# Two buffers for the weights of the wavelet layer's products, paid for with the GpSimd descriptor ring

## The chip, the cores and the metric

The kernel runs on one core of one Trainium2 chip. The metric is the device time of one execution in microseconds. Three executions of the kernel before took 18142.69, 18163.43 and 18164.18 us; the median is 18163.43 us.

A core has TensorE (PE in the profile; PEld is its loading of weights), VectorE (DVE), ScalarE (ACT), GpSimd (POOL) and SyncE (SP). All work from fast memory of 128 partitions (SBUF); products go to PSUM. Each engine takes its own instructions in order. SP and POOL start transfers; 16 DMA engines carry them.

## The reference

The input is `x` of 8 images, 64 channels, 128 x 128, float32. Four layers follow each other, each as `x = x + layer(groupnorm(x))`:

```python
x = x + relu(b - sum |patch - w|)         # layer 0: 3x3 "adder" convolution, 64 channels out
x = x + scale * silu(x) + spline(x)       # layer 1: per channel, B-spline
x = x + idwt(gelu(conv3x3(conv1x1(dw3x3(haar(x))))))   # layer 2: wavelet layer, 256 channels at 64 x 64
x = x + embed[argmin |x - embed|^2]       # layer 3: nearest of 512 vectors
```

Layer 0 has no product in it: for each output it sums 576 absolute differences.

## The kernel before

**Pairs.** Two images (64 channels each) fill the 128 partitions, so there are four pairs. Layer 0 is by far the longest. For pair 0 it runs alone; then one long run of layer 0 does pairs 1, 2 and 3, and beside it the layers 1, 2 and 3 of the pair before are done in small steps (`beside`, L1736). The last pair's layers 1 to 3 come at the end with nothing beside them.

**Layer 0** (L548 on). A tap is one shift of a 32-row chunk against one output channel's weight. ACT makes `|x - w|` of a tap (L821), or DVE makes `max(x, w)` (L774) and may fold a second and third tap into it (L844); PE sums the tile over channels into PSUM with a selection matrix (L809). A tile is 128 x 4096 floats, 16 KB of a partition. While the program is built, `layer0` keeps a clock of each engine from fixed costs, hands taps to ACT or DVE by it, and so writes the order of all engines out by hand; nothing of it is decided while the chip runs. There is a second way to fold two DVE taps, the *merge* (L832): POOL starts a transfer that adds one tile to another in SBUF (`accum_op=ALU.add`), 2 MB, and PE later takes the sum. The policy `ALONE` (pair 0) merges; `BESIDE` has its threshold `merge_free` at 99 and never does. After each pass of 144 taps ACT writes `y` (L645), eight POOL transfers add the layer's input to it (`residual`, L658, 64 KB each), and SP stores it (L673). The planner counts a merge as landed 12.5 us after it begins (`MERGE`), and plans its use by PE 5 or 9 us after that (`SETTLED`, `UNSETTLED`).

**Layer 2 beside layer 0** (`layer2_beside`, L1416). `spread_out` runs events by step: `at(step, f, ...)`. There are 514 steps to a pair, and chunks of 16 rows that are 56 steps apart. For chunk `c` that begins at step `b`, PE does sixteen groups of 24 matmuls (`products`, L1507, the matmuls at L1516), with the steps `b + 14 * at_m + 3 + 3 * n`: four kinds of product `at_m`, four groups each, three steps between groups of a kind and five from one kind to the next. Each group needs its own 384 KB of weights, tile `u2`, loaded from DRAM by SP (`load_u2`, L1503, L1505). The profile writes this tile as `u`. The pool has `bufs=1`, so there is one `u2` tile in this layer: a load waits until the group before it is done with the tile. A load stands one step behind the group before its own; the first of a chunk stands at `b - 3`.

**SP's queue.** SP is not ordered by hand, but takes its transfers in the program's order, and one that waits holds those behind it. In this layer these are the input rows `xin` (L1456, one buffer, free when DVE's `rows` of the part before are done), the residual rows `xa` (L1563, stored at L1579 after DVE's `add`), layer 0's stores of `y` (L673, each waiting for `residual` to land), small ones for layer 0's linear part (L621, L631, L635), and the weights (L1505).

**POOL's transfers.** Merges, `residual` and layer 3's gathers (L1687, L1245) go through POOL, which writes their descriptors into a ring in SBUF. `dynamic_dma_scratch_size` is the ring's size in bytes of each partition: 4096.

Of the kernel before, what the change touches and what calls it, by code (L numbers as in the profile page):

```python
# [13 lines left out]
F32 = mybir.dt.float32  # L14
# [7 lines left out]
P = 128  # L22
# [76 lines left out]
class Net:  # L99
# [1316 lines left out]
    def layer2_beside(self, stats_in, stats, steps):  # L1416
# [3 lines left out]
        nc, tc = self.nc, self.tc  # L1420
# [6 lines left out]
        def at(step, f, *a):  # L1427
            events[step].append((f, *a))

        with ExitStack() as ctx:  # L1430
            sp = ctx.enter_context(tc.tile_pool(name="b2", bufs=1))
# [20 lines left out]
            xins, vs, mms, gs, pys, u2s, xas = {}, {}, {}, {}, {}, {}, {}  # L1452
# [48 lines left out]
                nc.vector.tensor_tensor(vs[c, m], d[a], d[z], op)  # L1501

            def load_u2(c, m, oab, half):  # L1503
                t = u2s[c, m, oab, half] = sp.tile([P, 2, 3, P], F32, name="u2")
                nc.sync.dma_start(out=t, in_=self.u2_dram[:, oab, m, 2 * half : 2 * half + 2])  # L1505

            def products(c, m, oab, half):  # L1507
# [76 lines left out]
            for j in range(NCH + 1):  # L1584
                b, each = (7, LEAD) if j == 0 else (7 + LEAD + EACH * (j - 1), EACH)
                if j < NCH:
                    lo, row = (2 * G * j + 4, 2) if j else (0, 0)
                    hi = min(2 * G * (j + 1) + 4, H)
                    for h, s in enumerate((-5, -2, 1, 4) if j else range(0, 10, 2)):
                        to = min(lo + G // 2, hi)  # L1590
                        if lo == to:
                            continue
                        at(max(b + s - 3, 0), load, j, h, lo, to)
                        at(b + s + 1, columns, j, h, to - lo)
                        if h == 0 and j > 0:
                            at(b + s + 2, halo, j)
                        at(b + s + 2, rows, j, h, to - lo, row)
                        row += (to - lo) // 2
                        lo = to
                    for n in range(36):  # L1600
                        at(b + 7 + n * (each - 10) // 36 if j else b + 11 + n * (each - 14) // 36, depthwise, j, n)
                    at(b + each - 2, border, j)
                if j >= 1:
                    c = j - 1
                    kinds = ((1, take_first), (0, take_second), (2, take_third), (3, take_fourth))
                    when = [(b + 14 * at_m + 3 + 3 * n, c, m, n // 2, n % 2) for at_m, (m, _) in enumerate(kinds) for n in range(4)]
                    for n, (step, *what) in enumerate(when):
                        at(when[n - 1][0] + 1 if n else b - 3, load_u2, *what)
                        at(step, products, *what)
                    for at_m, (m, take) in enumerate(kinds):  # L1610
                        at(b + 14 * at_m, columns_of, c, m)
                        at(b + 14 * at_m + 15, take, c)
                    for oab in range(2):
                        at(b + 58, gelu, c, oab)
                    for a in range(2):
                        s = b + 60 + 9 * a
                        at(s - (8 if a == 0 else 1), load_x, c, a, 0)
                        for n in range(2):
                            at(s + n, inverse, c, 2 * a + n)
                        for h in range(2):  # L1620
                            for n in range(2):
                                at(s + 3 + 4 * h, add, c, 2 * a + n, h)
                            at(s + 3 + 4 * h, store, c, a, h)
                        at(s + 4, load_x, c, a, 1)
# [165 lines left out]


# [13 lines left out]
```

## Time and profile before

| | us |
|---|---|
| median of three executions | 18163.43 |
| profiled execution, whole | 18174.13 |
| its span, first to last instruction | 18172.4 |
| PE busy | 17725.0 (98%) |
| DVE busy | 17665.0 (97%) |
| ACT busy | 17155.7 (94%) |
| POOL busy | 3450.7 (19%) |
| pair 0, layer 0 alone | about 160 to 3640 |
| layer 0 of pairs 1 to 3, other layers beside it | about 3640 to 16900 |
| of that, matmuls of `products` | 4706 to 6140, 9200 to 10990, 13760 to 15516 |
| last pair's layers 1 to 3 | about 16900 to 18172 |

"Busy" counts time in which an engine runs an instruction; idle time is put down to what ended it, "who waited for whom". For PE and DVE all idle time together is 447 and 507 us of the span, and it comes in single waits of some microseconds. A row of the timeline gives start, duration, engine, line, operation, tiles and, in brackets, the idle time before it with its releaser.

### The profile page before, as it was taken

How to read it: one execution, taken by the hardware profiler on the slowest of the kernel's cores; microseconds unless marked ns; L12 is line 12 of the kernel's file. 1: busy time of each engine (PE TensorE's matmuls, PEld its weight loads, DVE VectorE, ACT ScalarE, POOL GpSimd, SP SyncE). 2: the span in 40 equal slices, each digit the busy share in tenths (PEclk: the TensorE clock that was granted, in tenths of full speed). 3: DMA queues.
4: the chain of work that ended last, by engine and by line, in shares of the span. 5: the costliest groups of instructions: out<-in, count | busy, mean ns of one | idle time of the engine just before them, and what ended most of it. 6: DMA issues, size and time to landing. Idle time of an engine off the chain costs nothing.

```text
span 18172.4 us, 338264 instructions
## 1 busy us (share of the span) xinstructions
PE 17725.0 (98%) x150466; PEld 6115.0 (34%) x150466; DVE 17665.0 (97%) x13415; ACT 17155.7 (94%) x6554; POOL 3450.7 (19%) x1866
## 2 busy tenths in 40 slices
PE   8999999999999999999999999999999999999999
PEld 2222222222333332332233333333223333333365
DVE  8999999999999999999999999999999999999998
ACT  7999999999999999999999999999999999999925
POOL 1222222200000024440000002453000000244305
PEclk9999999999999999999999999999999999999998
DMA  6767767711111110011111111001111111110231
GB/s 144 133 125 137 137 126 127 145 43 39 44 49 52 45 41 26 23 32 36 40 43 48 51 46 41 26 23 32 39 41 41 48 53 43 29 29 21 61 103 56
DMA packets 454215, 1099.93 MB, mean 61 GB/s; under 512 B 72416, under 2 KB 234848, under 8 KB 395360
## 3 DMA queue, kind: packets, MB, share of 16 engines
q0 software_dynamic: 111792, 491.89, 15.2%
q1 hardware_dynamic: 340960, 586.39, 11.1%
q8 instruction: 1179, 19.32, 0.4%
q14 instruction: 284, 2.33, 0.0%
HBM read 526.58 MB, written 125.74 MB: 36 GB/s over the span
## 4 chain that ended last, share of the span: by engine, by line
PE 51%; DVE 27%; issue 11%; ACT 8%; DMA 2%; POOL 0%; SPq 0%; DVEq 0%; ACTq 0%; POOLq 0%
PE ps L809 39%; DVE buf L774 13%; ACT buf L821 6%; DVE buf L844 4%; PE mm L1516 4%; PE pd L1672 1%; PE m L1080 1%; DVE dw L1489 1%; DVE wide L774 1%; DVE r L1358 1%; DMA buf<-buf 1%; PE ps L1230 1%; DVE x L844 1%; DVE x L774 1%; ACT t L1674 1%
## 5 line engine op out<-in xcount | busy, mean ns | idle before, releaser
L809 PE MATMUL ps<-buf,sel 128*32 128x512 f32 x112944 | 12564.7, 594 | 142.6 <-ACT buf L821 57.8
L821 ACT ACTIVATE buf<-wide,w 128x4096 f32<-128x4096 f32 x1898 | 6918.7, 3724 | 58.1 <-PE ps L809 57.6
L821 ACT ACTIVATE buf<-x,w 128x4096 f32<-128x4096 f32 x1820 | 6637.6, 3717 | 76.8 <-PE ps L809 71.9
L809 PEld LDWEIGHTS ps<-buf,sel 128*32 128x32 f32 x112944 | 3547.9, 110 | 8589.2 <-issue 7829.1
L774 DVE TENSOR_SCALAR buf<-x,w 128x4096 f32<-128x4096 f32 x1807 | 4183.6, 2358 | 55.5 <-PE ps L809 45.4
L774 DVE TENSOR_SCALAR buf<-wide,w 128x4096 f32<-128x4096 f32 x1737 | 4041.4, 2368 | 34.8 <-PE ps L809 30.6
L1687 POOL DMA_INDIRECT g<-in_L_conv_embed_weight,ix x768 | 1885.3, 2455 | 2322.9 <-issue 1188.2
L658 POOL DMA_DIRECT2D y<-in_x x496 | 702.9, 2230 | 6852.5 <-ACT y L645 5454.4
L844 DVE SCALAR_TENSOR_TENSOR buf<-x,w,buf 128x4096 f32<-128x4096 f32 x417 | 1870.2, 4485 | 14.8
L844 DVE SCALAR_TENSOR_TENSOR buf<-wide,w,buf 128x4096 f32<-128x4096 f32 x409 | 1834.2, 4485 | 14.5
L1516 PE MATMUL mm<-v,u 64*128 64x256 f32 x9216 | 1147.1, 393 | 76.2 <-DMA u<-u_dram 60.3
L832 POOL DMA_DIRECT2D buf<-buf x203 | 546.5, 2694 | 2713.2 <-DVE buf L774 2321.0
L1516 PEld LDWEIGHTS mm<-v,u 64*128 64x128 f32 x9216 | 871.9, 190 | 485.2 <-issue 299.4
L821 ACT ACTIVATE x<-wide,w 128x4096 f32<-128x4096 f32 x266 | 990.2, 3722 | 6.4 <-PE ps L809 6.4
L821 ACT ACTIVATE wide<-x,w 128x4096 f32<-128x4096 f32 x260 | 966.7, 3718 | 2.8 <-PE ps L809 2.7
L809 PE MATMUL ps<-x,sel 128*32 128x512 f32 x7760 | 928.3, 594 | 4.8 <-DVE x L844 4.4
L809 PE MATMUL ps<-wide,sel 128*32 128x512 f32 x7664 | 917.2, 593 | 8.5 <-ACT wide L821 5.5
L1489 DVE SCALAR_TENSOR_TENSOR dw<-sub,dws,dw 128x512 f32<-128x512 f32 (+2 forms) x768 | 573.5, 747 | 11.0
L1674 ACT ACTIVATE t<-emb,xsq 128x512 f32<-128x512 f32 x768 | 516.6, 727 | 39.1 <-DVE best L1684 28.7
L1684 DVE CUSTOM_DVE_ANT_0 nd<-pd,t 128x512 f32<-128x512 f32 x768 | 520.2, 677 | 23.2 <-ACT t L1674 14.3
L1686 DVE FIND_INDEX8 ix<-best,nd 128x8 uint32<-128x512 f32 x768 | 526.4, 685 | 0.1
L774 DVE TENSOR_SCALAR wide<-x,w 128x4096 f32<-128x4096 f32 x219 | 516.8, 2360 | 6.6 <-PE ps L809 6.6
(286 smaller groups left out, 10591.1 us busy)
## 6 DMA issues: line engine op xcount, KB each, us to landing
buf<-buf POOLq DMA_DIRECT2D x203, 2048.0 KB, 15.7
u<-u_dram SPq DMA_DIRECT2D x512, 384.0 KB
z<-x_dram SPq DMA_DIRECT2D x192, 256.0 KB
x<-x_dram SPq DMA_DIRECT2D x96, 512.0 KB
raw<-in_x SPq DMA_DIRECT2D x32, 1024.0 KB
x_dram<-y SPq DMA_DIRECT2D x512, 64.0 KB
y<-in_x POOLq DMA_DIRECT2D x496, 64.0 KB, 5.1
x_dram<-x SPq DMA_DIRECT2D x48, 512.0 KB
```

Source lines behind the costliest of these rows:

```text
L658: nc.gpsimd.dma_start(out=ys[p][at], in_=d, accum_op=ALU.add)
L774: nc.vector.tensor_scalar(ab, tap(p // OG, t), w[:, t : t + 1], None, ALU.max)
L809: nc.tensor.matmul(to, sel[:, M - 1 - m : 3 * M - 1 - m], rhs, start=(done % TAPS == 0), stop=((done + span) % TAPS == 0))
L821: nc.scalar.activation(ab, tap(p // OG, t), AF.Abs, bias=w[:, t : t + 1], scale=-1.0)
L832: nc.gpsimd.dma_start(out=into, in_=of, accum_op=ALU.add, max_dma_last_dim=8192)
L844: nc.vector.scalar_tensor_tensor(ab, tap(p // OG, t), w[:, t : t + 1], ab, ALU.max, ALU.add)
L1489: nc.vector.scalar_tensor_tensor(out, v, wt, out, ALU.mult, ALU.add)
L1516: nc.tensor.matmul(ps[:, i], u2[r, k % 2, di, :], vs[c, m][r, k, di : di + G, :], start=(k == 0 and di == 0), stop=(k == 3 and di == 2))
L1674: nc.scalar.activation(t, emb[:, 1], AF.Identity, bias=xsqs[j][:, n : n + 1])
L1684: nc.vector.tensor_tensor_reduce(nd, ps, t, 1.0, -FAR, ALU.subtract, ALU.max, mx[:, 0:1])
L1686: nc.vector.max_index(ix, mx, nd)
L1687: nc.gpsimd.indirect_dma_start(out=g[:, img, :], out_offset=None, in_=self.embed, in_offset=bass.IndirectOffsetOnAxis(ap=ix[:, 0:1], axis=0),)
```

## The change

`u2` gets two buffers in the layer beside layer 0. Each load moves one group ahead: it stands one step behind the group two before its own, and the first two of a chunk stand at `b - 5` and `b - 4`. A buffer is 2 x 3 x 128 floats, 3072 bytes of a partition. The ring of POOL's descriptors goes from 4096 to 1024 bytes of a partition, which frees 3072.

```diff
             def load_u2(c, m, oab, half):
-                t = u2s[c, m, oab, half] = sp.tile([P, 2, 3, P], F32, name="u2")
+                t = u2s[c, m, oab, half] = sp.tile([P, 2, 3, P], F32, name="u2", bufs=2)
                 nc.sync.dma_start(out=t, in_=self.u2_dram[:, oab, m, 2 * half : 2 * half + 2])
...
                     for n, (step, *what) in enumerate(when):
-                        at(when[n - 1][0] + 1 if n else b - 3, load_u2, *what)
+                        at(when[n - 2][0] + 1 if n > 1 else b - 5 + n, load_u2, *what)
                         at(step, products, *what)
...
-    nc = bacc.Bacc("TRN2", target_bir_lowering=False, num_devices=1, dynamic_dma_scratch_size=4096)
+    nc = bacc.Bacc("TRN2", target_bir_lowering=False, num_devices=1, dynamic_dma_scratch_size=1024)
```

## The prediction

> **What bounds the kernel now.** First the stretches of the two stages that the change touches: layer 0 alone (pair 0), where all merges are, and the three stretches with `products`.
>
> ```profile
> 160.00:3640.00 3480.00, 3428.33 (x31548) 1018.77 (x31540) 3422.90 (x1429) 3409.49 (x969) 773.28 (x332) 1.00 0.73 132
> 4706.00:6140.00 1434.00, 1413.91 (x12520) 562.05 (x12520) 1419.94 (x887) 1404.40 (x419) 47.41 (x44) 0.99 0.18 50
> 9200.00:10990.00 1790.00, 1756.43 (x15503) 694.74 (x15502) 1757.96 (x1055) 1739.24 (x517) 59.42 (x52) 0.99 0.17 47
> 13760.00:15516.00 1756.00, 1728.04 (x15300) 688.04 (x15292) 1735.15 (x1030) 1720.15 (x511) 75.78 (x58) 0.99 0.17 48
> ```
>
> After each length come the busy times of PE, PEld, DVE, ACT and POOL. PE and DVE are both about 98.5% busy: PE idles 52 us of the first stretch and 82 us of the other three together, DVE 57 and 67. The reader is to see that neither stage has one bound: time given to PE counts only as far as DVE was waiting for it. So I read the waits next: PE's, DVE's for the time beside other layers (3640 to 16900), and POOL's neighbours.
>
> ```profile
> PE mm L1516 <- DMA u<-u_dram: 60.3, 28, 6.7
> PEld mm L1516 <- DMA u<-u_dram: 90.1, 33, 7.6
> PE ps L809 <- DMA buf<-buf: 28.7, 5, 10.5
> ...
> DVE buf L774 <- PE ps L809: 48.9, 26, 14.8
> ```
>
> Of 384 groups of `products`, 33 start late because their weights have not landed; PE idles 60 us there. The merges already cost PE 28.7 us. Then the timeline at one of the 33:
>
> ```profile
> 9649.29 2.41 PE L1516 MATMUL mm<-v,u 64*128 64x256 f32 x20
> 9659.25 0.32 SPq L1456 DMA_DIRECT2D xin<-x_dram  x1
> 9659.67 0.37 SPq L1505 DMA_DIRECT2D u<-u_dram  x1
> 9662.93 4.55 PE L1516 MATMUL mm<-v,u 64*128 64x256 f32 x24 [4.23 <-DMA u<-u_dram]
> ```
>
> The buffer was free at 9651.7, but SP stood before `xin`, whose buffer DVE freed at 9659.2; the weights went out behind it and landed 3.2 us later. The 24 matmuls then take 4.55 us in place of 2.86: after a long wait PE runs slow for a while. Last the merges:
>
> ```profile
> L832 POOL DMA_DIRECT2D buf<-buf x203: 1201/2211/22579, 141.2 to 3599.1; - x102
> DMA to landing us min/median/max: 14.6/15.7/35.2
> ...
> 1386.31 1.95 POOL L832 DMA_DIRECT2D buf<-buf  x1 [13.88 <-PE ps L809]
> 1399.79 2.21 POOL L832 DMA_DIRECT2D buf<-buf  x1 [11.53 <-DVE buf L774]
> ...
> q0 software_dynamic: 272, 2.10, 81.2%
> ```
>
> A merge lands 15.7 us after POOL begins it, and here the next begins after 13.5 us. The last line is the window of one merge, 1388 to 1402.5: 272 packets, which by size are 256 of 8192 B and 16 of 4 B, 17 for each of 16 DMA engines.
>
> **Part 1, the loads: -25 us.** Each load moves one group ahead in SP's queue. Groups follow each other by 8.7 us (median, never under 5.2), so a load that is now issued 3.2 us ahead of its matmuls, as the latest are, has at least 8.4 us even if SP is as late as before; it needs 3.2. Mostly SP is not late: in 12 of the 33 the transfer just ahead is `xin`, in 10 the `xa` loads and stores, in 8 layer 0's `y` stores, and the load now stands before most of them. I take all 33 as gone. On PE they are worth 60 us idle and, summed over the same groups, 23 us of slow matmuls (length above 2.83 us). What a load now waits for, the group two before, is done a step before the load's place, as was the group before in the old order, so it holds SP no longer than now; the exception is a chunk's second load, two steps ahead of the end of the group whose buffer it takes (before, the first load stood one step ahead). A step is about 3.9 us (13260 us for three pairs of 1142 steps), and what stands there, `xa` rows due eight steps later, covers it. I count nothing; without that cover it would be 24 chunks by 3.9 us, 94 us.
> How much of the 83 us reaches the end: 21 of the 33 lie on the chain that ended last, with 52 us of idle and 20 us of slow matmuls, so 71 is the upper bound. DVE, which is as full, waits for PE in the three stretches only 31 us (buf 3.1 + 17.9 + 7.9, x 1.0 + 0.6). With PE on time DVE is late next, and it can't gain more than it waits. I take 25, between nothing and 71, nearest to DVE's row.
> The slow matmuls can be held against a rule. All 11 groups behind an idle of 2.40 us or more are slow, and none behind 2.36 or less by over 0.5 us. The Trainium skill, TensorE: Matmul & The Clock Gate, Part 1, puts the fall of the clock behind an idle window of about 3.4 us; by it only the 6 groups above that would be slow, some 13 us and not 23. The row decides, and the 25 stays in either case, since DVE sets it.
>
> **Part 2, the ring: +65 us.** The trace of before shows no wait for the ring, so its price is bounded from both sides. With a quarter of the ring either nothing waits (0; a gain is excluded, as no work goes away), or two merges no longer fit together, and each must wait until the one before has landed.
> Which of the two: the trace shows the ring of 4096 B with two merges in it at most; a quarter of it must hold one for the program to run, and no row shows that it holds two. A merge reads both operands: an 8192 B packet of a plain load takes 309 ns (median of 5168 DMA records), one of a merge 672 ns. If each read has an entry of its own, a merge takes 16 x 2 + 1 = 33 entries of each engine's ring; if each packet has one, 17. I take the first, by the doubled time, and so the wait.
> The skill's DMA: Bandwidth & Descriptors (Terms; SWDGE vs HWDGE vs iDMA) gives 16 B a descriptor and one read and one write descriptor for each operation. By that, which no run here shows, a ring of 1 KB would hold 64, three merges of 17 would fit, this part would cost 0 and the sum would be that of rival 1.
> If they wait: by the DMA records (end of a merge's last 8192 B packet) 117 of the 203 merges begin before the one before has landed, by 1.3 us in the median. Their data moves 2.21 + 0.57 us after POOL begins (issue, first packet), so only 15 now find the DMA engines busy; with the wait, those 2.8 us follow the landing and all 117 come later. Between landing and PE's use lie 7.3 us in the median, 5.6 in the lower quarter, 3.3 in the lowest tenth. One merge alone is harmless. But a merge needs 12.2 us from first packet to landing, and 12.2 + 2.8 = 15.0 is longer than the 13.5 us between merges in tight runs, so lateness adds up, 1.5 us each. Going through the 203 in order with the trace's times, PE's own delay added to all that follows: 18 come late for 53 us if POOL sees the landing at once, 31 for 68 us if 0.3 us after, 43 for 94 us if 0.6 us after. I take 68, plus 7 for slow matmuls after long waits, less 10: PE now waits 18.7 us in this stretch for tiles of DVE, and I count half of that as overtaken. Behind a waiting merge stand `residual` transfers; eight in a pass are due at least 12 taps before their use, some 21 us, and are hidden. Beside other layers there is no merge, and gathers and `residual` are far apart (256 gathers to 396 steps of 3.9 us, 6 us each); the end's gathers land in 2.4 us and go out every 0.95 us, so few are in flight. No price there.
>
> **Sum.** The profiled execution took 18174.13 us (span 18172.4), 10.7 above the median of 18163.43. 18174 - 25 + 65 = 18214; on the median 18203.
>
> **Rivals.**
> 1. The ring has room (17 entries a merge). For: merges overlap by 1 to 3 us only, and other bookkeeping is possible. Against: doubled packet time. Then 18163 - 25 = 18138, and 18092 if all 71 us on the chain come through. This is the other side; it decides from a gain of 36 us on.
> 2. The ring costs more: POOL sees a landing 1 us late, so that in the same going-through 55 merges are late for 139 us, or 164 with no transfer under 12.2 us. 18163 - 25 + 140 = 18278 or so. For: 7.3 us of margin is used up quickly in runs. Against: PE's waits give the DMA engines time to catch up.
> 3. The loads were hidden anyway: DVE's 31 us turn up at another place of its chain. 18163 + 65 = 18228.
>
> **How the numbers follow.** 0.2% is 36 us, about what a measurement of this kernel can tell from no change. The forecast (both parts, 18175 to 18248) has 0.44, split 0.20 within and 0.24 above; rival 1 has 0.28 (0.13 faster, 0.15 within), rival 2 0.15 (slower), rival 3 0.13 (0.02 within, 0.11 slower). Faster 0.13, same 0.37, slower 0.50. The range 18125 to 18290 leaves out 0.12 of rival 1 and 0.08 of rival 2.
>
> **What would show it.** Loads: PE's wait for `u` near 0, L1505 issued ahead of `xin`, DVE's waits for PE in the three stretches well under 31 us. Ring: POOL's merges wait for, or last until, the landing of the one before; PE's wait for merges 60 to 110 us in place of 28.7; the first stretch longer by about 65 us. A first stretch of unchanged length proves rival 1. The forecast is wrong by more than its range if gathers meet the ring too, or if a held SP queue makes `xin` late for DVE (10.6 us now).

## The result and the profile after

The changed kernel takes 18239.37 us (median of five, 18213.04 to 18275.06) and the kernel before 18161.26 us (median of five, 18142.69 to 18164.18). The ratio is 1.0047, with a 95% interval of 1.0036 to 1.0058: 78 us slower by the medians, 85 by the ratio. The profiled execution of the changed kernel took 18213.04 us and is the fastest of its five, so its trace shows only 39 us of the loss; the two parts of the change are nevertheless plain in it.

The stretches first, laid by the same marks as before (the end of pair 0's layer 0, the same instructions of `products`). After each length come the busy times of PE, PEld, DVE, ACT and POOL, then the granted clock.

```profile
160.00:3723.00 3563.00, 3443.68 (x31532) 1019.63 (x31524) 3417.39 (x1429) 3408.67 (x968) 760.93 (x332) 0.99 0.71 129
4790.00:6224.00 1434.00, 1420.90 (x12616) 565.70 (x12614) 1424.16 (x890) 1412.35 (x422) 49.88 (x44) 1.00 0.18 50
9270.00:11040.00 1770.00, 1750.57 (x15504) 693.83 (x15492) 1756.02 (x1054) 1736.85 (x517) 59.94 (x52) 1.00 0.17 48
13805.00:15556.00 1751.00, 1727.33 (x15312) 687.23 (x15304) 1733.66 (x1030) 1719.08 (x511) 72.63 (x58) 1.00 0.17 47
```

ACT's last `y` of pair 0 comes at 3720.3 us in place of 3637.6: the first stretch is 82.7 us longer. PE idles 119 us there (3563 less 3443.7) where it idled 52, and its busy time is 15 us longer, at a clock of 0.99 in place of 1.00. From the first to the last matmul of `products` the three pairs take 1722.8, 1702.2 and 1736.4 us in place of 1731.2, 1722.0 and 1742.8, 34.6 us less together. (The first pair's `products` go on to 6437 in the trace of before, not to 6140 as the table and the window in the prediction have it; the whole of it is meant here.) Everything else together is 9 us shorter. 82.7 - 34.6 - 9 is the 39 us of the trace.

Next the merges: POOL's line for them, its timeline at the place that the prediction showed, and the waits of the first stretch, of before and then after.

```profile
L832 POOL DMA_DIRECT2D buf<-buf x203: 1201/2159/16654, 139.7 to 3691.5; - x102
...
DMA to landing us min/median/max: 13.8/15.7/25.7
```

```profile
1389.52 1.22 POOL L832 DMA_DIRECT2D buf<-buf  x1 [13.32 <-issue]
1403.95 1.82 POOL L832 DMA_DIRECT2D buf<-buf  x1 [13.21 <-DMA buf<-buf]
1420.08 2.17 POOL L832 DMA_DIRECT2D buf<-buf  x1 [14.31 <-DVE buf L774]
```

```profile
POOL buf L832 <- DVE buf L774: 2230.4, 164, 41.1
POOL buf L832 <- DMA buf<-buf: 95.1, 7, 15.2
...
DVE buf L774 <- PE ps L809: 27.0, 29, 5.6
```

```profile
POOL buf L832 <- DVE buf L774: 1086.6, 73, 41.2
POOL buf L832 <- issue: 724.7, 57, 14.9
POOL buf L832 <- DMA buf<-buf: 589.5, 45, 15.8
...
PE ps L809 <- DMA buf<-buf: 104.8, 33, 10.7
DVE buf L774 <- PE ps L809: 90.4, 60, 8.2
...
DVE stats_first L455 <- DMA y<-in_x: 24.9, 3, 21.6
...
PE ps L809 <- DVE buf L774: 10.1, 8, 7.1
```

Before, POOL's merges waited for DVE's tiles 164 times of 203 and for a landing 7 times. Now 102 of them wait for the landing of the one before, or for nothing that the profile shows ("issue"). By the DMA records 117 merges began before the previous one had landed; now none does. 167 of 203 begin 0.5 to 1.0 us after that landing, the earliest 0.59 us. Between a merge's landing and PE's use of it lay 7.3 us in the median; now it is 3.95, and 38 merges land when PE already stands at their use, which then follows within 0.6 us (4 before). PE's wait for merges goes from 28.7 to 104.8 us, and DVE, whose buffers PE frees later, waits 90 us for PE in place of 27.

From its beginning to its landing a merge takes 15.7 us in the median, as before: as a rule it is not slower, it begins later. But some are held in POOL besides, with their data not yet moving: the records of twelve last 5.5 to 16.7 us in place of 2.2 (eight in the trace of before, up to 22.6). PE's waits for eleven of the twelve make up 61 of its 105 us; in the trace of before four held merges make up 25 of the 28.7. The last section shows what these records have in common. So about half of the rise by 76 us is merges that come late and are held as well.

The loads, SP's and PE's timelines around the group that the prediction showed (a row of several instructions covers the time from the first to the last, waits included):

```profile
9646.06 22.47 SPq L1505 DMA_DIRECT2D u<-u_dram  x3
9678.22 9.74 SPq L673 DMA_DIRECT2D x_dram<-y  x8
9688.05 0.37 SPq L1505 DMA_DIRECT2D u<-u_dram  x1
```

```profile
9643.15 2.86 PE L1516 MATMUL mm<-v,u 64*128 64x256 f32 x24
...
9654.67 2.86 PE L1516 MATMUL mm<-v,u 64*128 64x256 f32 x24
...
9665.30 2.86 PE L1516 MATMUL mm<-v,u 64*128 64x256 f32 x24
...
9676.82 2.86 PE L1516 MATMUL mm<-v,u 64*128 64x256 f32 x24
```

Each of these four groups runs in 2.86 us with no wait in front; of the 33 late groups none is left that costs PE time. Not all of PE's idle time before groups goes: what the profile puts down to "issue" there grows from 12.6 to 35.3 us, so that with the 60.3 us for weights gone PE idles 32 us less at the groups' first matmuls. A load is issued 22.1 us ahead of its matmuls in the median (8.6 before), never under 8.4. DVE's waits for PE in the three stretches fall from 31.7 to 5.3 us; most of them lay in the second, whose rows are these, before and after:

```profile
DVE buf L774 <- PE ps L809: 17.9, 11, 6.8
```

```profile
DVE buf L774 <- PE ps L809: 0.6, 1, 0.6
```

### The profile page after: what moved, and what is told of

Read it like the earlier page. It is cut to its first block, busy times and chain, and to the rows that moved or that the text cites. A ratio compares the mean times of both kernels' runs of the same rounds, so it can differ in the third digit from the quotient of the medians.

```text
span 18211.3 us, 338282 instructions
## 1 busy us (share of the span) xinstructions
PE 17732.2 (97%) x150466; PEld 6115.2 (34%) x150466; DVE 17633.2 (97%) x13415; ACT 17145.2 (94%) x6554; POOL 3693.6 (20%) x1866
## 4 chain that ended last, share of the span: by engine, by line
PE 53%; DVE 24%; issue 12%; ACT 7%; DMA 3%; POOL 1%; SPq 0%; DVEq 0%; ACTq 0%; POOLq 0%
PE ps L809 40%; DVE buf L774 12%; ACT buf L821 5%; PE mm L1516 5%; DVE buf L844 4%; DMA buf<-buf 2%; PE m L1080 1%; PE pd L1672 1%; DVE r L1358 1%; PE ps L1230 1%; DVE wide L774 1%; DVE dw L1489 1%; DVE nd L1684 1%; ACT t L1674 1%; DVE x L774 1%
## 5 line engine op out<-in xcount | busy, mean ns | idle before, releaser
L809 PE MATMUL ps<-buf,sel 128*32 128x512 f32 x112944 | 12584.9, 595 | 207.1 <-DMA buf<-buf 104.8
L1687 POOL DMA_INDIRECT g<-in_L_conv_embed_weight,ix x768 | 2147.4, 2796 | 2061.2 <-issue 984.4
L1516 PE MATMUL mm<-v,u 64*128 64x256 f32 x9216 | 1135.4, 390 | 43.8 <-issue 35.3
L821 ACT ACTIVATE wide<-x,w 128x4096 f32<-128x4096 f32 x260 | 964.8, 3711 | 11.8 <-PE ps L809 11.7
## 6 DMA issues: line engine op xcount, KB each, us to landing
buf<-buf POOLq DMA_DIRECT2D x203, 2048.0 KB, 15.7
```

The source lines that it names most:

```text
L809: nc.tensor.matmul(to, sel[:, M - 1 - m : 3 * M - 1 - m], rhs, start=(done % TAPS == 0), stop=((done + span) % TAPS == 0))
L821: nc.scalar.activation(ab, tap(p // OG, t), AF.Abs, bias=w[:, t : t + 1], scale=-1.0)
L1516: nc.tensor.matmul(ps[:, i], u2[r, k % 2, di, :], vs[c, m][r, k, di : di + G, :], start=(k == 0 and di == 0), stop=(k == 3 and di == 2))
L1687: nc.gpsimd.indirect_dma_start(out=g[:, img, :], out_offset=None, in_=self.embed, in_offset=bass.IndirectOffsetOnAxis(ap=ix[:, 0:1], axis=0),)
```

## The experiments

Ten kernels, in three groups that shared a chip and its executions of the kernel before. Chips differ: the kernel before had a median of 18225.5 us with the first four and 18226.2 with the last two, 18159.3 with the middle four. The trace shows where: with the first four, the stage behind the last pass of layer 0 (from 17121 us in the trace of before, not from 16900 as the table has it) is 1113 to 1118 us long, against 1051 in the trace of before, whatever the kernel, and PE's granted clock from 17700 to 18160 us is 0.78 and 0.81 (runs 3 and 4) in place of 0.88. So times are compared as ratios to the kernel before on the same chip, and stretches between traces of one group. "Faster" and "slower" in us are worked out from the ratio; where a difference of medians is meant, the text says so.

**1. The ring alone.** The kernel before, one buffer, old places.

```diff
-    nc = bacc.Bacc("TRN2", target_bir_lowering=False, num_devices=1, dynamic_dma_scratch_size=4096)
+    nc = bacc.Bacc("TRN2", target_bir_lowering=False, num_devices=1, dynamic_dma_scratch_size=1024)
```

> The kernel before with the ring at 1024 B and nothing else changed; one buffer for the weights, loads where they were. Theory A (two merges no longer fit in 1024 B, since a merge takes 33 entries of each DMA engine's ring): all of the loss is here and the gain of the loads (34.6 us in the three stretches with products) is missing, so 78 + 35 = about 113 us slower than before, 80 to 130; the first stretch 83 us longer than 3477.6 us, no merge begun before the one before has landed, PE's wait for merges about 104 us. Theory B (part of the loss comes from the moved loads, or from the place where tiles lie): the first stretch is clearly less than 83 us longer and the whole under 60 us slower.

Measured: 18335.58 us, ratio 1.0057 (1.0043 to 1.0071), 104 us slower (110 by the medians). The first stretch ends at 3724.7 us, 104 us behind that of run 4 on the same chip; no merge begins before a landing. The waits of its first stretch:

```profile
POOL buf L832 <- DVE buf L774: 995.6, 67, 41.2
POOL buf L832 <- issue: 739.8, 57, 14.9
POOL buf L832 <- DMA buf<-buf: 670.2, 51, 16.3
...
PE ps L809 <- DMA buf<-buf: 102.6, 35, 9.9
```

The picture is that of the changed kernel, with the loads where they were. The whole loss is the ring's (theory A); the expected 113 lies in the interval.

**2. Sixty-four bytes more.** As 1, with `dynamic_dma_scratch_size=1088`.

> The kernel before with the ring at 1088 B, 64 B more than in the change. Theory A (33 entries a merge; the Trainium skill, DMA: Bandwidth & Descriptors, Terms, gives 16 B a descriptor): 64 more bytes let two merges of 33 in, so merges begin before the one before has landed again, in about 100 of 203 cases, PE's wait for merges falls from 104 to under 50 us, and the whole is 0 to 40 us slower than before; what is left are the five or so residual transfers of a pass that no longer fit beside two merges. Theory C (a short ring costs in proportion to its size, for instance by the work of writing it round its end): nearly the same as with 1024 B, 80 us or more slower, and no sudden change.

Measured: 18225.14 us, ratio 0.9999 (0.999 to 1.0008). 99 of 203 merges begin before the landing of the one before, and the waits are nearly back at what they were:

```profile
POOL buf L832 <- DVE buf L774: 2153.5, 157, 41.2
POOL buf L832 <- issue: 120.3, 15, 13.6
POOL buf L832 <- DMA buf<-buf: 96.2, 8, 14.1
...
PE ps L809 <- DMA buf<-buf: 19.3, 8, 10.1
```

Nearly all of the price goes in one step, at the size that the count of 33 entries names, and not in proportion to the size (theory C falls). A little stays: with 1088 B (runs 2 and 5) 29 merges begin 0.5 to 1.0 us after a landing, against 9 to 12 in the traces with 1536 or 4096 B, and the first stretch ends at 3627 and 3630 us, against 3618 to 3621 with 1536 B (runs 3, 4 and 7).

Two merges need more than 1024 and at most 1088 B of ring, so one needs more than 512 and at most 544 if the whole ring can be filled; 32 entries with a place or more that must stay free would show the same step, and no run tells these apart. The Trainium skill, DMA: Bandwidth & Descriptors, Terms, gives a descriptor 16 B; estimated by it, that is 33 or 34 descriptors, and with 17 a merge three would have fitted in 1024. The skill has the missing half on another page, Collectives: The Full Stack, in the section on the bandwidth ceiling: there the adding step of a ReduceScatter emits two read descriptors for each chunk, since it has two sources. That a merge does the same is a reading from the step and from the doubled packet time; no run shows it directly.

**3. Two buffers and a ring that holds two merges.** The changed kernel with `dynamic_dma_scratch_size=1536`.

> The changed kernel, two buffers and moved loads, with the ring at 1536 B in place of 1024. Theory A: two merges and some residual transfers fit, the ring costs 0 to 10 us, and the loads' 35 us remain: 18161 - 35 = 18126 us, 18110 to 18150, faster than before; first stretch within 10 us of 3477.6, begun merges before the landing about 117. Theory D (the loads' gain in the stretches is given back elsewhere): within 10 us of before, although the three stretches are 30 us shorter. Theory C: still 40 us or more slower than before in the first stretch.

Measured: 18181.85 us, ratio 0.9975 (0.9965 to 0.9984), 46 us faster than before. Theory A; its 35 us lie in the interval (29 to 64 us). The first stretch ends at 3618.4 us, 19 us ahead of the first trace and not within 10 of it as expected; run 8 shows why.

**4. One buffer with the same ring.**

> The kernel before with the ring at 1536 B and nothing else changed. Theory A: within 10 us of before, and the difference to the run with two buffers and the same ring is what the loads are worth, about 35 us. Theory C: 40 us or more slower than before.

Measured: 18212.11 us, ratio 0.9992 (0.9983 to 1.0002); PE waits 15.1 us for merges. Between runs 3 and 4 only the buffer and the places of the loads differ: 30.3 us by the medians. The loads' gain is real and is given back nowhere. Theory D falls.

**5. The change with 64 B more.** The changed kernel with `dynamic_dma_scratch_size=1088`.

> The changed kernel with 64 B more of ring, 1088 in place of 1024, two buffers and moved loads as they are. Theory A (a merge takes 33 entries, so 1024 B misses two merges by two entries): the whole loss of the first stretch goes, merges overlap in about 100 of 203 cases, PE's wait for merges is under 50 us, and the loads' gain remains: 30 to 45 us faster than before, ratio 0.9970 to 0.9985. Theory E (the two parts hinder each other with a short ring): within 15 us of before or slower.

Measured: 18123.23 us, ratio 0.9982 (0.9973 to 0.9991), 33 us faster than before; 97 merges overlap, PE waits 19.7 us for them. 64 bytes of ring are the difference between 0.47% slower and 0.18% faster.

**6. The short ring, and a planner that knows of it.** The changed kernel with its 1024 B:

```diff
-MERGE, SETTLED, UNSETTLED = 12.5, 5.0, 9.0
+MERGE, SETTLED, UNSETTLED = 15.5, 5.0, 9.0
```

> The changed kernel with its ring of 1024 B, and the planner told that a merge occupies 15.5 us (landing 12.1 after the first packet, 2.16 + 0.57 from the beginning to the first packet, 0.65 from the landing to the next beginning) in place of 12.5. Theory A (the loss is lateness that the planner does not know of): PE's wait for merges falls from 104 to under 40 us, fewer merges than 203 are written (about 190) and each one missing costs DVE 2.1 us (a fold of 4.48 in place of a tile of 2.36), so half or more of the loss goes: 0 to 45 us over the before, with the loads' gain included. Theory F (the ring itself makes each merge slower or POOL's waiting holds others): PE's wait for merges stays above 70 us and the time within 20 us of the changed kernel's (78 us over before).

Measured: 18125.83 us, ratio 0.9982 (0.9973 to 0.9991), 33 us faster than before. The planner writes 176 merges. None begins before the previous landing and 16 still wait for one by the profile, but PE's use is planned late enough:

```profile
POOL buf L832 <- DMA buf<-buf: 209.6, 16, 16.6
POOL buf L832 <- issue: 204.0, 17, 14.9
...
PE ps L809 <- DMA buf<-buf: 13.6, 2, 9.4
```

The price of fewer merges is small: in the first stretch 18 more folds (18 x 4.485 = 81 us of DVE), 24 fewer tiles of `max(x, w)` (24 x 2.36 = 57 us) and 6 more taps on ACT; the stretch ends at 3635.2 us, against 3623.5 for the kernel before on this chip (run 8). So the short ring is slow because the order written out counts on merges 12.5 us apart, not because the data of a merge moves more slowly. Six merges are held here, in place of twelve. Theory A, and more of the loss goes than it expected.

**7. Two buffers, the loads at their old places,** with 1536 B of ring. Against the changed kernel the loads move back:

```diff
-                        at(when[n - 2][0] + 1 if n > 1 else b - 5 + n, load_u2, *what)
+                        at(when[n - 1][0] + 1 if n else b - 3, load_u2, *what)
```

> Two buffers and a ring of 1536 B, but the loads at their old places, one step behind the group before their own. Tells apart which half of the change makes the loads punctual. Theory G (SP's queue: the load stands behind xin, xa and the stores): a second buffer alone helps little, 20 or more of the 33 late groups stay, and the time is within 15 us of the kernel before with this ring (0.9992). Theory H (the wait for the one buffer): fewer than 10 late groups, and the time is that of the run with moved loads, 0.9975.

Measured: 18121.08 us, ratio 0.9979 (0.997 to 0.9988), 38 us faster than before. No group is late. Theory H: the second buffer alone makes the loads punctual, and the move by one group is worth nothing that was measured (run 3: 0.9975, run 5: 0.9982; the three stretches 5162 us long, against 5165 and 5163). SP's timeline over some 31 us:

```profile
9555.63 10.96 SPq L1505 DMA_DIRECT2D u<-u_dram  x2
9576.32 9.73 SPq L673 DMA_DIRECT2D x_dram<-y  x8
9586.14 0.37 SPq L1505 DMA_DIRECT2D u<-u_dram  x1
```

and of the kernel before on the same chip (run 8), around the place that the prediction showed:

```profile
9654.80 0.32 SPq L1456 DMA_DIRECT2D xin<-x_dram  x1
9655.22 0.37 SPq L1505 DMA_DIRECT2D u<-u_dram  x1
9661.52 0.32 SPq L1456 DMA_DIRECT2D xin<-x_dram  x1
9669.58 0.32 SPq L1505 DMA_DIRECT2D u<-u_dram  x1
```

A place is only an order in SP's queue. With one buffer a load goes out no earlier than PE is done with the group before (0.04 us behind it in the median), and what else stands in the queue comes on top. With two it waits for the group two before instead and goes out 11.7 us ahead of the end of the group before (median, at either place), so that a transfer that holds the queue for some microseconds no longer makes the weights late.

**8. The kernel before once more,** for a trace from the chip of runs 5 to 7.

> The kernel before, for a trace from the same chip as the runs above: ratio 1.000. If 4096 and 1536 B are the same to the program, its first stretch ends at 3615 to 3632 us, as with 1536 (3620.7) and 1088 (3627.1), and its last stage is some 1115 us long, 62 more than on the chip of the first trace. If more ring is harmful, its first stretch ends at 3637 again.

Measured: ratio 1.0001 (0.9991 to 1.0011). The first stretch ends at 3623.5 us, PE waits 16.1 us for merges. So in time 4096 B are no better or worse than 1536 or 1088, and the trace of before that the prediction read (3637.6 and 28.7) was 14 us worse than this one in this stretch. PE's waits for held merges are 25 us there and 13 here. The last stage is 1053.5 us long, not the 1115 expected: this chip is not the one of runs 1 to 4.

**9 and 10. Without `residual`.** In pair 0, where the merges are, the transfers that add the layer's input are left out, with 1024 and with 1536 B of ring. Against the kernel before, beside the size of the ring:

```diff
-                    nc.gpsimd.dma_start(out=ys[p][at], in_=d, accum_op=ALU.add)
+                    if len(pairs) > 1: nc.gpsimd.dma_start(out=ys[p][at], in_=d, accum_op=ALU.add)
```

> The kernel before with a ring of 1024 B and without layer 0's residual transfers in pair 0 (the layer's input is not added there, fifteen of sixteen passes; pairs 1 to 3 keep theirs). Against the run without residual and 1536 B it gives the price of the short ring that merges alone pay. Theory M (merges alone, one behind the other, seen 0.65 us after landing): the difference is as large as with residual, 118 us by the medians and 104 by the first stretches. Theory R (residual transfers behind a waiting merge add to it: DVE's one wait of 21.6 us for a residual lay on the chain): the difference is smaller by about 20, 95 us by the medians and 83 by the first stretches, and no wait of DVE for a residual is left.

> The same without residual transfers in pair 0, with a ring of 1536 B. Both theories: within 15 us of the run with 1536 B and residual (0.9992 of before), since there DVE waits for a residual only 2.0 us and the planner doesn't count them; first stretch 3605 to 3622 us.

The reason for them: in the trace after, and in that of run 1, `residual` was not hidden. At 1977 us DVE starts its statistics 21.6 us late; in run 1 the chain that ended last passes through the same place:

```profile
1968.97 0.46 POOL buf L832
1969.43 0.29 issue
1969.72 15.30 DMA y<-in_x
```

The last of six transfers goes out 0.75 us behind a waiting merge and lands with it. Measured without them: 18329.75 us, ratio 1.0049 (1.0035 to 1.0063), and 18220.1 us, 0.9995 (0.9986 to 1.0004). The ratios differ by 98 us, where they differed by 118 with `residual`; the medians by 110, where they differed by 123; the first stretches by 118.1, where they differed by 104.0. DVE's wait is gone, and PE waits 113.5 us for merges:

```profile
PE ps L809 <- DMA buf<-buf: 113.5, 28, 12.6
```

Theory R wanted 20 us less. It is 20 less by the ratios, 14 less by the medians and 14 more by the first stretches, and the executions of runs 1 and 9 alone lie 71 and 54 us apart: these runs don't decide between M and R. A delay of 21.6 us on the chain was there; whether it cost time stays open. The merges alone pay 98 to 118 us by these measures.

## Why the prediction was right, and where it was off

**Which way.** 18203 us was forecast (18175 to 18248 for the likeliest case); 18239 was measured. Both mechanisms are as forecast: two merges no longer fit, as they would not with two entries for each piece, and this costs more than the loads bring. Run 2 shows the first by its step, runs 1 and 4 that the ring and nothing else costs, runs 3 and 4 what the loads bring. By the medians of the runs on their chips the sum is 110 - 30 = 80 us, against 78 measured for the whole change; by the ratios it is 104 - 31 = 73, against 85. Forecast was 65 - 25 = 40. Both terms were too small, and since they have opposite signs, 5 to 10 us of the error of the second were made up for by the first.

**Part 2, 65 us: the term that was mis-sized.** Measured: 83 us between the first traces, 97 against the trace of run 8, 104 by run 1. Two of its steps were too small, and one thing is missing in it.
- "I take 68", the value for a landing that POOL sees after 0.3 us. The prediction gives no row for 0.3. POOL goes on 0.6 to 0.7 us after the landing: the quarter and median of the distances are 0.65 and 0.71 us in the trace after, 0.64 and 0.70 in run 1. The prediction's own row for 0.6 us has 94. PE's wait for merges rises by 76 us between the first traces, and by 87.5 between runs 4 and 1; both lie between these rows. The row for the true reaction would have been 6 to 18 us too high in its turn, so that 68 was nearer than its reason.
- What the count left out. It goes by the times of the trace of before, in which eight merges are held. Twelve were held now, and PE's waits for held merges rise from 25 to 61 us; that merges which begin later lie differently against DVE's tiles is not in the prediction.
- "7 for slow matmuls after long waits." PE's busy time of the first stretch grows by 15 us between the first traces and by 24 between runs 4 and 1 (3448.7 less 3424.3), with a granted clock of 0.99 in place of 1.00. By the clock records of the traces PE ran at half speed for 96 us of this stretch, where it was 31 before (85 in run 1, 17 in run 4), and its waits of over 0.15 us for merges are 33 in place of 5.
- "Less 10" for waits on DVE that are overtaken was about right: PE's other idle time in this stretch falls by 8.5 us.

Besides, the trace that the sum was made against has a first stretch 14 us longer than the other trace of the same program (run 8). The profiled times agree with the sum of 18214 by accident: the executions of the changed kernel lie 62 us apart, and the profiled one is the lowest.

**Rival 2 (seen 1 us late, 140 us)** was too high and in the right direction: the true reaction lies between the value taken and this one. **Rival 1 (the ring has room)** fell with run 1; the first stretch is its proof, as the prediction said. **Rival 3 (the loads hidden anyway)** fell with runs 3 and 4.

**"`residual` ... due at least 12 taps before their use, and are hidden"** was wrong as a statement: one of them came 21.6 us late on the chain. Whether that cost time, runs 9 and 10 leave open.

**Part 1, 25 us.** All 33 late groups went, as taken. The gain is 34.6 us between the first traces, 35.3 from run 8 to run 5, and 30.3 by the medians of runs 4 and 3. DVE's waits for PE went from 31.7 to 5.3 us, 26 of the 35; so the rule that DVE can't gain more than it waits gave the right order where the chain's 71 us would have been twice too much. The other 7 us are DVE's busy time in the three stretches, 5128 to 5121 us; why its instructions take less is not settled. "It holds SP no longer than now" is right: SP stands 2426 us before these loads in the trace after, and 2644 in that of before, and DVE waits 12.9 us for `xin` in place of 10.6. No gain or loss of the place was found (run 7). Wrong was the reason for the punctuality, "the load now stands before most of them": not the place but the wait for the one buffer held the loads.

The limit that the prediction read for slow matmuls, between 2.36 and 2.40 us of idle, holds for its one trace. In run 8, the same program, late groups behind 2.48, 2.67, 2.71 and 3.63 us kept their 2.86 us, and one behind 2.70 took 4.24; in run 4 one behind 2.22 us took 4.55. Neither 2.4 us nor the 3.4 that the prediction sets against it is a sharp limit here. The 25 did not rest on it.

**No price beside other layers and at the end** holds: of the stages outside the first stretch and the three with `products`, none is longer in the trace after by more than 1.2 us.

## What to carry to other kernels

In this kernel the price of a smaller ring followed not its size but, to within some ten us, the number of the largest requests that fit in it at once. So count the entries of one request, and see whether a few bytes keep the second one in. If room must be found, look for the smallest size that still holds that number (here 1088 B in place of 1024 turned a loss into a gain), or tell the planner the longer distance. A late load with one buffer is first a matter of the buffer; where it stands in the queue comes after.

## What the runs showed of the hardware that was not expected

- With 1024 B the next merge begins 0.58 us after a landing at the earliest; the quarter and the median of the distances are 0.65 and 0.71 us in the trace after. In the profile the wait for room has no single name: it is idle time of POOL put down to "issue", to the landing or to a DVE tile.
- A merge's record can last far longer than its 2.2 us, and that is another wait. In run 1 the merge at 1405.56 begins 0.87 us after the landing of the one before, so the room is there; but its first packet moves only at 1421.5. DVE runs twelve tiles of `max(x, w)` back to back meanwhile, up to 1420.60. POOL's rows, then DVE's:

```profile
1391.08 1.22 POOL L832 DMA_DIRECT2D buf<-buf  x1 [13.32 <-issue]
1405.56 15.35 POOL L832 DMA_DIRECT2D buf<-buf  x1 [13.26 <-DMA buf<-buf]
1433.75 1.22 POOL L832 DMA_DIRECT2D buf<-buf  x1 [12.84 <-issue]
```

```profile
1393.36 27.24 DVE L774 TENSOR_SCALAR buf<-wide,w 128x4096 f32<-128x4096 f32 x12
1421.15 2.35 DVE L774 TENSOR_SCALAR x<-wide,w 128x4096 f32<-128x4096 f32 x1 [0.56 <-PE ps L809]
```

In the twelve traces 76 merge records last over 5 us. Every one ends 0.31 or 0.32 us after the end of a tile of `max(x, w)`, the last of a row without a gap: behind it DVE folds, takes statistics or stands idle. But of the 114 merges of the trace after that begin with over 4 us of such a row still to come, 102 are not held so. What decides which are held, and whether another order on DVE would free them, no run tested.

- With late merges the executions of one kernel spread: 62, 71 and 54 us between the lowest and the highest of five (the changed kernel, runs 1 and 9). With 1088 B or more, and with spaced merges on 1024 B (run 6), it is 10 to 32 us in up to eleven. Lateness that adds up from merge to merge, or a different set of held merges, would do this; it was not traced execution by execution.
- The same program differs by 66 us between chips. In the traces the difference lies behind the last pass of layer 0 (1113.0 us in run 4, 1053.5 in run 8). From 17850 us on the granted clock is 0.78 in run 4 and 0.88 in run 8, and POOL idles 65.5 us with "issue" before its gathers in place of 26.8; whether one of the two causes the other is not known.
